# A two-layer graph network with residual norms: the gates' layer norm cut in two, evictions and copies dealt out anew, and a tile of its own for row sums

## The chip, the cores and the metric

The kernel runs on one core of a Trainium2 chip. The core has a matrix engine (TensorE, PE in the profile), a vector engine (VectorE, DVE), a scalar engine (ScalarE, ACT), GpSimd (POOL) and a sync engine (SyncE, SP) that here only issues transfers. Each engine works through its own queue of instructions in order. The metric is the device time of one launch in microseconds (us), as the median of several runs; lower is better.

## The reference

There are 64 graphs of 256 nodes with 256 features, all in float32. Two layers follow each other, each with a residual sum and a layer norm without gain and bias:

```python
# layer 0
deg = adj.sum(-1);  d = where(deg != 0, deg, 1) ** -0.5
h   = (d[:, :, None] * adj * d[:, None, :] + alpha * eye) @ x
x   = layernorm(x + h @ W.T + b)

# layer 1, with mask = adj
h      = relu(bn1(conv1(x)));  h = bn2(conv2(h))        # conv2 has 17 taps along the nodes
x_conv = relu(h + x)
s      = x @ w_se.T + b_se                              # 3 columns
A      = exp(-|s_n - s_m|^2) * adj
x_nmp  = A @ relu(x @ w_msg.T + b_msg)
gi, gh = [x_conv, x_nmp] @ w_ih.T + b_ih,  x @ w_hh.T + b_hh
r, z   = sigmoid(gi_r + gh_r), sigmoid(gi_z + gh_z)
n      = tanh(gi_n + r * gh_n)
x      = layernorm(x + (1 - z) * n + z * x)
```

## The kernel before, in words

The graphs are taken in four blocks of 16 (`Q` = 16, `NQ` = 4). Each graph passes three stages.

**Layers.** `layer0(g)` makes row sums of adj, its transpose, and the first layer. The row sums (`degrees()`, L356) are ScalarE copies of adj whose accumulators are kept and whose copied values go into a part of the tile `adjT` that is overwritten later; `adjT` has three buffers, and its last reader of an earlier graph is the product with the exponentials (L508). `layer1(g, place)` makes from the norm's output the transposed input `xn` (`x1_transposed`, L430 on VectorE and L431 on ScalarE, out of one PSUM bank), the first convolution (p_conv, L446), messages (L467), the forward transform of 32 + 16 node windows (p_dft, L482) into the big tile `V`, the distances (`dist_l` on ScalarE, L497, and `dist_r` on VectorE, L499, out of one bank), and the product with the masked exponentials (p_nmp, L515).

**Transform.** The 17-tap convolution of a block is done in the frequency domain. `products(step)` multiplies the block's tile by tables streamed from DRAM (p_k, L541), `real_transform`, `complex_begin` and `complex_end(q)` are the inverse transform, nearly all VectorE, which ends with transfers to `xc_d` (L729).

**Gates.** `gru(g)` makes the gates as a block product with seven multiplications (p_g, L856) whose operands are sums formed by GpSimd (`input_sums`, L838). VectorE joins the products (L873, L874, L882, L884, L921), ScalarE applies tanh (L897, L913), and `finished(part)` joins the gates with x1 and ends with the layer norm and the output transfer (L917). `layernorm` is a generator in two parts: statistics, and the power -0.5 on GpSimd (L328); then, after a `yield`, the negative mean times scale on VectorE (L331) and two ScalarE activations (L333). `layer0` uses the pause in it; `finished` does not: `run(layernorm(...))` issues both parts at once. `load_x1(g)` (L794) loads the residual into one of two buffers, from which the output is also stored. For some graphs (`in_blocks`) VectorE transposes the convolution's result (L812) and GpSimd adds to it (L813), for the others TensorE transposes it (L822).

The blocks overlap. The first graphs of a block (`AHEAD`: 12 of the second block, 6 of the third and fourth) run their layers while the block before is still in the transform. As `V` is in use by then, they write into a second tile `V2`, and `copies(V2)` moves their columns into `V` once the inverse transform is done (L1086). The 12 graphs of the second block are the set `ALONE`: no gates run beside them, and each calls `x1_transposed` for the graph after it, ahead of its own p_nmp. While the inverse transform and these graphs run together, `paced` issues pieces of the transform behind certain marked instructions at rates written by hand; `issue_after` ties an instruction behind another of its engine. Otherwise the planner of the framework orders each engine's instructions by program order and by when their inputs are ready in its own model, so an instruction may be issued before others that stand above it in the text. It also allots the buffers and places all waits; two engines that read one PSUM bank are kept apart.

The gates of 12 of a block's 16 graphs run during the next block's transform (`late`), the first four during the layers (`early`). The last block's gates have nothing beside them but the transform, and at the very end nothing.

Of the kernel before, what the change touches and what calls it, by code (L numbers as in the profile page):

```python
# [9 lines left out]
F32 = mybir.dt.float32  # L10
# [4 lines left out]
P = 128  # L15
# [11 lines left out]
def kernel(  # L27
# [63 lines left out]
    def mark(op, gates=0):  # L91
        marks.append((op.ins, gates))
# [24 lines left out]
    alpha_t = const.tile([P, 1], F32)  # L117

    vectors = const.tile([16, P], F32, name="bn_in")
    neg_half = const.tile([P, 4], F32)  # L120
    nc.vector.memset(neg_half, -0.5)
    load(0)
# [223 lines left out]
    def layer0(g):  # L346

        a_t, x_t = ain.pop(g), xin.pop(g)

        adjT = work.tile([P, NCH, 3, P], F32, name="adjT", bufs=3)  # L350
        ADJT[g] = adjT

        deg = small.tile([P, NCH], F32, name="deg")
        def degrees():
            for c in range(NCH):
                nc.scalar.activation(  # L356
                    adjT[:, c, 0:2, :].rearrange("p n q -> p (n q)"), a_t[:, c, :], AF.Copy,
                    accum_out=deg[:, c : c + 1],
                )

        if g == 1:

            with tc.issue_after(X_SCALED[0]):
                degrees()
        else:
            degrees()
        nc.vector.scalar_tensor_tensor(deg, deg, 0.0, deg, op0=ALU.is_equal, op1=ALU.add)  # L367
        dis = small.tile([P, NCH], F32, name="dis")
        nc.gpsimd.tensor_tensor(dis, deg, neg_half[:, :NCH], op=ALU.pow)  # L369
        adeg = small.tile([P, NCH], F32, name="adeg")  # L370
        nc.vector.tensor_scalar(adeg, deg, alpha_t, None, op0=ALU.mult)

        p = bank("p_adjT").rearrange("p (c n) -> p c n", c=NCH)
        for mc in range(NCH):
            for c in range(NCH):
                nc.tensor.transpose(p[:, mc, c * P : (c + 1) * P], a_t[:, c, mc * P : (mc + 1) * P], ident)
        copied = nc.scalar.copy(adjT[:, :, 0:3:2, :], p.rearrange("p c (n q) -> p c n q", q=P))
        for mc in range(NCH):  # L380
            DIAGONAL[g] = nc.vector.scalar_tensor_tensor(
                adjT[:, mc, 1, :], ident, adeg[:, mc : mc + 1], adjT[:, mc, 2 * mc, :],
                op0=ALU.mult, op1=ALU.add,
            ).ins


        x1 = work.tile([P, NCH, D], F32, name="x1")
        X1[g] = x1
        with tc.issue_after(copied.ins) if g < 2 else ExitStack():
            for c in range(NCH):  # L390
                X_SCALED[g] = nc.scalar.activation(x1[:, c, :], x_t[:, c, :], AF.Copy, scale=dis[:, c : c + 1]).ins
        nc.gpsimd.tensor_tensor(x_t, x_t, b0_t.unsqueeze(1).to_broadcast([P, NCH, D]), op=ALU.add)

        yield
        hT = work.tile([P, DCH, N], F32, name="hT", bufs=1)
        p = bank("p_hT").rearrange("p (k n) -> p k n", k=DCH)
        for k in range(DCH):
            for mc in range(NCH):
                nc.tensor.matmul(  # L399
                    p[:, k, :], x1[:, mc, k * P : (k + 1) * P],  # L400
                    adjT[:, mc, 1 - mc : 3 - mc, :].rearrange("p n q -> p (n q)"),
                    start=mc == 0, stop=mc == NCH - 1,
                )
        nc.scalar.copy(hT, p)  # L404
        yield
        p = bank("p_out0").rearrange("p (c o) -> p c o", c=NCH)
        for c in range(NCH):
            for k in range(DCH):
                nc.tensor.matmul(  # L409
                    p[:, c, :], hT[:, k, c * P : (c + 1) * P], w0[:, k, :], start=k == 0, stop=k == DCH - 1  # L410
                )
        for c in range(NCH):
            mark(
                nc.vector.scalar_tensor_tensor(
                    x1[:, c, :], p[:, c, :], dis[:, c : c + 1], x_t[:, c, :], op0=ALU.mult, op1=ALU.add
                )
            )
        yield
        yield from layernorm(x1)
        nc.scalar.dma_start(x1_d[g // Q][g % Q].rearrange("(c p) d -> p c d", p=P), x1)  # L420
        yield

    def x1_transposed(g):
        x1 = X1.pop(g)
        xn = XN[g] = work.tile([P, 2 * DCH, N], F32, name="xn")
        p = bank("p_x1T").rearrange("p (k n) -> p k n", k=DCH)
        for k in range(DCH):
            for c in range(NCH):
                nc.tensor.transpose(p[:, k, c * P : (c + 1) * P], x1[:, c, k * P : (k + 1) * P], ident)
        nc.vector.tensor_scalar(xn[:, 0], p[:, 0], others_only, unit, op0=ALU.mult, op1=ALU.add)  # L430
        nc.scalar.copy(xn[:, 2 * DCH - 1], p[:, 1])  # L431

    def layer1(g, place):
# [62 lines left out]
        dl = work.tile([64, N], F32, name="dist_l", bufs=1)  # L496
        nc.scalar.copy(dl, p[0:64, :N])  # L497
        dr = work.tile([64, N], F32, name="dist_r", bufs=1)
        nc.vector.tensor_copy(dr, p[64:P, :N])  # L499
        yield  # L500

        aT = work.tile([P, NCH, 2, P], F32, name="aT", bufs=1)
# [5 lines left out]
        mark(nc.vector.tensor_mul(aT, aT, adjT[:, :, 0:3:2, :]))  # L508
        yield
        if g in ALONE:  # L510
            x1_transposed(g + 1)
        p = bank("p_nmp").rearrange("p (k n) -> p k n", k=DCH)
        for k in range(DCH):
            for mc in range(NCH):
# [277 lines left out]
    def load_x1(g):  # L792
        OWN[g] = gate.tile([P, NCH, D], F32, name="x1_g")
        nc.sync.dma_start(OWN[g], x1_d[g // Q][g % Q].rearrange("(c p) d -> p c d", p=P))  # L794
# [35 lines left out]
    def input_sums(g, *which):  # L830
        A11, A12, A21, A22 = halves(GATE[g])
        S = SUMS.setdefault(g, {})
        for i in which:
# [3 lines left out]
            }[i]  # L837
            nc.gpsimd.tensor_tensor(S[i], x, y, op=op)  # L838

    def gru(g):  # L840


# [19 lines left out]
        def quarter(c, h):  # L862
            return G[:, c, h].rearrange("p t d -> p (t d)")
# [13 lines left out]
        yield  # L877
        if following:
            transposed(g + 1)
        load_x1(g)  # L880
        p5 = product(S[1], T1)
        mark(nc.vector.tensor_add(quarter(1, 1), quarter(1, 1), p5), 1)  # L882
# [18 lines left out]
        def finished(part):  # L901
            both = G[:, part].rearrange("p c h t d -> p (c h) t d")
            chunks = both.shape[1] // 2
            r, z, n, i = (both[:, :, j, :] for j in (GR, GZ, GN, GI))
            nc.vector.scalar_tensor_tensor(n, r, 1.0, n, op0=ALU.add, op1=ALU.mult)  # L905
            i4 = i.rearrange("p (c h) d -> p c h d", h=2)
            bias = bn_t.rearrange("p (h d) -> p h d", h=2).unsqueeze(1).to_broadcast([P, chunks, 2, HD])
            nc.vector.tensor_tensor(i4, i4, bias, op=ALU.add)
            nc.vector.scalar_tensor_tensor(i, n, 0.5, i, op0=ALU.mult, op1=ALU.add)
            y = x1[:, part]  # L910
            yq = y.rearrange("p c (h d) -> p (c h) d", h=2)
            mark(nc.vector.scalar_tensor_tensor(yq, z, 3.0, yq, op0=ALU.add, op1=ALU.mult), 1)
            nc.scalar.activation(i, i, AF.Tanh)  # L913
            nc.vector.scalar_tensor_tensor(i, z, 1.0, i, op0=ALU.subtract, op1=ALU.mult)
            nc.vector.tensor_sub(yq, yq, i)
            run(layernorm(y, 4 * LN_EPS))
            nc.scalar.dma_start(out[g].rearrange("(c p) d -> p c d", p=P)[:, part], y)  # L917

        if g == B - 1:
            finished(slice(1, 2))  # L920
        mark(nc.vector.tensor_add(quarter(0, 1), quarter(0, 1), p5), 1)  # L921
        squashed(0)
        finished(slice(0, 1 if g == B - 1 else NCH))
# [27 lines left out]
    def run(stage):  # L951
        for _ in stage:
            pass
# [103 lines left out]
    def gates(q, part):  # L1057

        for i in part:
            if i == 0:  # L1060
                load_conv(q * Q)
                load_gate(q * Q)
                yield
                load_conv(q * Q + 1)
                sent(q * Q)
                yield
                transposed(q * Q)
                yield
                input_sums(q * Q, 3, 1, 2, 4)
                yield  # L1070
            yield from gru(q * Q + i)
# [8 lines left out]
    def copies(V2):  # L1080

        waiting = list(AWAY)
        AWAY.clear()
        TILES[0] = V
        for i in waiting:
            nc.scalar.copy(V[:, :, :, i * GT : (i + 1) * GT], V2[:, :, :, i * GT : (i + 1) * GT])  # L1086
            yield

    late = nothing()
    for q in range(NQ):  # L1090
# [32 lines left out]
        if more:  # L1123
            run(late)
            run(end)
            if q == 0:
                scope.close()
                gate = ctx.enter_context(tc.tile_pool(name="gate", bufs=2))
            early = gates(q, range(EARLY))
            others = [take(early, 5 if q == 0 else 2) for _ in range(Q)]  # L1130
            run(graphs(first, range(AHEAD, Q), others))
            run(early)
            if q == 0:
                scope, AHEAD, V2 = open_ahead(6)
                ctx.enter_context(scope)
            late = gates(q, range(EARLY, Q))
        else:
            run(gates(q, range(Q)))
    order.close()


# [51 lines left out]
```

## Time and profile before

| | before |
|---|---|
| time, median of 3 runs | 2126.97 us (2122.22 to 2134.46) |
| the profiled execution | 2127.71 us, of which span 2125.9 us |
| TensorE busy (matmuls) | 2006.1 us, 94% of the span |
| VectorE busy | 1474.1 us, 69% |
| ScalarE busy | 905.3 us, 43% |
| GpSimd busy | 666.8 us, 31% |
| HBM, mean over the span | 139 GB/s |

The span is the time from the first to the last instruction of the program. Busy time counts the stretches in which an engine has at least one instruction running; matmuls overlap one another. A line such as L430 is a line of the kernel's file, printed with the functions above. "p_conv L446 <- DVE xn L430" says that the instruction on the left waited for the one on the right.

### The profile page before, as it was taken

To read this page: it belongs to the slowest core of one execution; us is meant where nothing else is said; L and a number is where in the kernel's file an instruction comes from. 1 tells how busy PE (TensorE), PEld (TensorE's weight loads), DVE (VectorE), ACT (ScalarE), POOL (GpSimd) and SP (SyncE) were. 2 spreads that over 40 slices of the span, in tenths; PEclk is the share of its full clock that TensorE was granted. 3 is DMA by queue.
4 is the path that set the end of the run, shared out by engine and by line. 5 is a ranking of instruction groups with operands and counts; after the bars stand their busy time and mean duration, and the time that the engine had idled before them with its cause. 6 is when DMAs were issued, how large, how long until landed. Compare 5 with 4: busy or idle time off the path is not lost. (4 is left out here: it accounts for less than half of the span.)

```text
span 2125.9 us, 26260 instructions
## 1 busy us (share of the span) xinstructions
PE 2006.1 (94%) x8157; PEld 1443.2 (68%) x8157; DVE 1474.1 (69%) x3347; ACT 905.3 (43%) x2114; POOL 666.8 (31%) x672
## 2 busy tenths in 40 slices
PE   6999999888999999999999999999999999899997
PEld 5888788766667756667777666667777765555554
DVE  5555567775558788774556888875445889977776
ACT  4666643456432234555553123446554123233333
POOL 3445310121431243223321234323232123344443
PEclk9999999999999999999999999999999999999999
DMA  4766556433437645344335655334323754443331
GB/s 125 230 210 200 192 183 209 154 132 119 122 96 226 194 123 139 114 120 120 94 99 179 201 155 140 118 104 134 96 93 100 243 146 131 111 118 95 93 94 56
DMA packets 305289, 298.05 MB, mean 140 GB/s; under 512 B 84192, under 2 KB 283956, under 8 KB 305150
## 3 DMA queue, kind: packets, MB, share of 16 engines
q1 hardware_dynamic: 245198, 200.37, 32.1%
q10 hardware_dynamic: 44480, 67.39, 8.9%
q0 software_dynamic: 15472, 28.61, 6.0%
q8 instruction: 66, 1.08, 0.2%
q14 instruction: 73, 0.60, 0.1%
HBM read 193.19 MB, written 103.06 MB: 139 GB/s over the span
## 5 line engine op out<-in xcount | busy, mean ns | idle before, releaser
L856 PE MATMUL p_g<-wall,sums 128*128 128x384 f32 x1536 | 537.7, 489 | 11.6 <-DVE G L882 11.6
L856 PE MATMUL p_g<-wall,inputs 128*128 128x384 f32 x1152 | 409.4, 492 | 14.5 <-DVE G L874 14.1
L856 PEld LDWEIGHTS p_g<-wall,sums 128*128 128x128 f32 x1536 | 284.6, 191 | 200.3 <-issue 19.1
L856 PEld LDWEIGHTS p_g<-wall,inputs 128*128 128x128 f32 x1152 | 218.5, 192 | 167.5 <-DVE G L874 23.4
L838 POOL TENSOR_TENSOR sums<-inputs 128x384 f32<-128x384 f32 x128 | 139.9, 1093 | 343.2 <-PE p_g L856 296.9
L369 POOL TENSOR_TENSOR dis<-deg,neg_half 128x2 f32<-128x2 f32 x64 | 48.3, 754 | 475.7 <-DVE deg L367 468.6
L897 ACT ACTIVATE G<-G 128x512 f32<-128x512 f32 x128 | 80.7, 630 | 250.8 <-DVE G L884 148.6
L328 POOL TENSOR_TENSOR ln_rs<-ln_rs,neg_half 128x2 f32<-128x2 f32 x129 | 94.9, 736 | 275.1 <-DVE ln_rs L327 226.7
L541 PE MATMUL p_k<-u,VM 128*128 128x256 f32 x736 | 175.8, 381 | 4.1 <-DMA u<-ud 4.1
L541 PEld LDWEIGHTS p_k<-u,VM 128*128 128x128 f32 x736 | 139.4, 191 | 31.3 <-DMA u<-ud 3.9
L446 PE MATMUL p_conv<-wc,xn 128*128 128x259 f32 x512 | 130.4, 392 | 22.7 <-DVE xn L430 21.5
L399 PE MATMUL p_hT<-adjT,x 128*128 128x256 f32 x512 | 126.7, 391 | 15.6 <-ACT msg L470 8.2
L333 ACT ACTIVATE x_g<-x_g,ln_mr,ln_rs 128x256 f32<-128x256 f32 x128 | 70.0, 593 | 150.3 <-DVE ln_mr L331 148.3
L446 PEld LDWEIGHTS p_conv<-wc,xn 128*128 128x128 f32 x512 | 94.2, 191 | 53.1 <-DVE xn L430 31.1
L508 DVE TENSOR_TENSOR aT<-aT,adjT 128x512 f32<-128x512 f32 x64 | 44.8, 699 | 123.0 <-ACT aT L507 122.8
L409 PE MATMUL p_out<-w,hT 128*128 128x256 f32 x512 | 123.7, 384 | 3.4 <-ACT hT L404 3.0
L482 PE MATMUL p_dft<-fwd,h 128*128 128x240 f32 x512 | 117.4, 372 | 9.2 <-ACT scols L450 8.8
L515 PE MATMUL p_nmp<-aT,msg 128*128 128x256 f32 x512 | 122.6, 383 | 0.7 <-DVE aT L508 0.7
L467 PE MATMUL p_msg<-wmsg,xn 128*128 128x256 f32 x512 | 122.0, 381 | 0.0
L838 POOL TENSOR_TENSOR sums<-inputs,sums 128x384 f32<-128x384 f32 x64 | 70.2, 1097 | 161.3 <-PE p_g L856 160.6
L331 DVE SCALAR_TENSOR_TENSOR ln_mr<-ln_mv,ln_rs 128x2 f32<-128x2 f32 x129 | 47.3, 368 | 101.7 <-POOL ln_rs L328 101.7
L409 PEld LDWEIGHTS p_out<-w,hT 128*128 128x128 f32 x512 | 95.6, 190 | 29.9 <-ACT hT L404 9.9
(160 smaller groups left out, 3642.0 us busy)
## 6 DMA issues: line engine op xcount, KB each, us to landing
u<-ud SPq DMA_DIRECT2D x284, 256.0 KB
xn_d<-xn ACTq DMA_DIRECT2D x64, 512.0 KB
inputs<-xn_d SPq DMA_DIRECT2D x64, 512.0 KB
ud<-u_set POOLq DMA_DIRECT2D x39, 480.0 KB, 6.3
adj_t<-in_adj_dram SPq DMA_DIRECT2D x64, 256.0 KB
x_t<-in_x_dram SPq DMA_DIRECT2D x64, 256.0 KB
x_d<-x ACTq DMA_DIRECT2D x64, 256.0 KB
xc_d<-VM SPq DMA_DIRECT2D x64, 256.0 KB
```

The source lines that it names most:

```text
L328: nc.gpsimd.tensor_tensor(rs[:, : len(chunks)], rs[:, : len(chunks)], neg_half[:, : len(chunks)], op=ALU.pow)
L333: nc.scalar.activation(y[:, c, :], y[:, c, :], AF.Identity, bias=mr[:, c : c + 1], scale=rs[:, c : c + 1])
L399: nc.tensor.matmul(p[:, k, :], x1[:, mc, k * P : (k + 1) * P], adjT[:, mc, 1 - mc : 3 - mc, :].rearrange("p n q -> p (n q)"), start=mc == ...
L409: nc.tensor.matmul(p[:, c, :], hT[:, k, c * P : (c + 1) * P], w0[:, k, :], start=k == 0, stop=k == DCH - 1)
L446: nc.tensor.matmul(p, x1T[:, k, c * P : (c + 1) * P], wc1[:, k, :], start=k == 0, stop=k == DCH - 1)
L467: nc.tensor.matmul(p[:, c, :], x1T[:, k, c * P : (c + 1) * P], wmsg[:, k, :], start=k == 0, stop=k == DCH - 1)
L482: nc.tensor.matmul(p[:, t0 * FL : t1 * FL], h[:, c, k * P : (k + 1) * P], fwd[:, first : first + t1 - t0, :].rearrange("p t f -> p (t f)") ...
L515: nc.tensor.matmul(p[:, k, :], msg[:, mc, k * P : (k + 1) * P], aT[:, mc].rearrange("p n q -> p (n q)"), start=mc == 0, stop=mc == NCH - 1,)
L541: nc.tensor.matmul(p[:, j * D : (j + 1) * D], v[:, k, :], u[:, k, :], start=k == 0, stop=k == DCH - 1)
L838: nc.gpsimd.tensor_tensor(S[i], x, y, op=op)
L856: nc.tensor.matmul(p[:, : 3 * HD] if k == 0 else p[:, HD:], a[:, k], wall[:, b, k].rearrange("p t d -> p (t d)"), start=first and k == 0, ...
L897: nc.scalar.activation(rz, rz, AF.Tanh, scale=0.5)
```

## The change

It has four parts. The row sums of adj write their unused copy into a tile of their own. In the graphs of `ALONE`, `x1_transposed` and the copy `dist_r` use ScalarE for the eviction that VectorE did. Of the copies from `V2` to `V`, every second one goes to VectorE. And the gates' layer norm is a generator `normed`, of which `finished` runs the first part; `ended()` runs what is left, together with the output transfer, from the next graph's gates, from the last graph between its two halves, and once after all.

```diff
     vectors = const.tile([16, P], F32, name="bn_in")
+    unused = const.tile([P, N], F32, name="unused")
...
         def degrees():
             for c in range(NCH):
                 nc.scalar.activation(
-                    adjT[:, c, 0:2, :].rearrange("p n q -> p (n q)"), a_t[:, c, :], AF.Copy,
+                    unused, a_t[:, c, :], AF.Copy,
                     accum_out=deg[:, c : c + 1],
                 )
...
-    def x1_transposed(g):
+    def x1_transposed(g, alone=False):
...
-        nc.vector.tensor_scalar(xn[:, 0], p[:, 0], others_only, unit, op0=ALU.mult, op1=ALU.add)
+        if alone:
+            nc.scalar.activation(xn[:, 0], p[:, 0], AF.Identity, bias=unit, scale=others_only)
+        else:
+            nc.vector.tensor_scalar(xn[:, 0], p[:, 0], others_only, unit, op0=ALU.mult, op1=ALU.add)
         nc.scalar.copy(xn[:, 2 * DCH - 1], p[:, 1])
...
-        nc.vector.tensor_copy(dr, p[64:P, :N])
+        if g in ALONE:
+            nc.scalar.copy(dr, p[64:P, :N])
+        else:
+            nc.vector.tensor_copy(dr, p[64:P, :N])
...
         if g in ALONE:
-            x1_transposed(g + 1)
+            x1_transposed(g + 1, True)
...
+    NORMS = []
+
+    def normed(g, part, y):
+
+        yield from layernorm(y, 4 * LN_EPS)
+        nc.scalar.dma_start(out[g].rearrange("(c p) d -> p c d", p=P)[:, part], y)
+
+    def ended():
+        while NORMS:
+            run(NORMS.pop(0))
+
     def gru(g):
...
         if following:
             transposed(g + 1)
+        ended()
         load_x1(g)
...
-            run(layernorm(y, 4 * LN_EPS))
-            nc.scalar.dma_start(out[g].rearrange("(c p) d -> p c d", p=P)[:, part], y)
+            NORMS.append(normed(g, part, y))
+            next(NORMS[-1])

         if g == B - 1:
             finished(slice(1, 2))
+            ended()
...
         for i in waiting:
-            nc.scalar.copy(V[:, :, :, i * GT : (i + 1) * GT], V2[:, :, :, i * GT : (i + 1) * GT])
+            copy = nc.vector.tensor_copy if i % 2 else nc.scalar.copy
+            copy(V[:, :, :, i * GT : (i + 1) * GT], V2[:, :, :, i * GT : (i + 1) * GT])
             yield
...
             run(gates(q, range(Q)))
+    ended()
     order.close()
```

## The prediction

> **What bounds the kernel now.** I read the busy shares first, then the windows by stage, then TensorE's waits inside the stages that lose time, and last the timeline of those places.
>
> ```profile
> span 2125.9 us, 26260 instructions
> ...
> PE 2006.1 (94%) x8157; PEld 1443.2 (68%) x8157; DVE 1474.1 (69%) x3347; ACT 905.3 (43%) x2114; POOL 666.8 (31%) x672
> ```
>
> TensorE is the bound: the whole change can win only what TensorE stands idle, 2125.9 - 2006.1 = 119.8 us. The first 50 us hold 50 - 32.4 = 17.6 us of it (loads and setup) and the tail after the last matmul 26.0 - 14.5 = 11.5 us. Neither is touched, so 90.7 us in the middle are at stake, 4% of the span. The windows (columns: window, its length, busy time of PE, PEld, DVE, ACT, POOL with instruction counts, clock, DMA) say where:
>
> ```profile
> 410.00:514.00 104.00, 91.16 (x444) 72.89 (x443) 79.60 (x233) 57.51 (x157) 20.73 (x22) 1.00 0.38 128
> 514.00:524.00 10.00, 3.87 (x18) 3.08 (x18) 0.62 (x5) 10.00 (x18) 0.89 (x2) 0.78 0.28 94
> 1745.00:1900.00 155.00, 140.94 (x440) 81.16 (x441) 140.13 (x271) 47.62 (x87) 58.80 (x59) 0.98 0.46 123
> 1900.00:2100.00 200.00, 197.85 (x612) 115.62 (x611) 144.84 (x264) 73.37 (x132) 95.65 (x104) 1.00 0.37 92
> ```
>
> The graphs of layers that run ahead (410 to 514) lose 12.8 us, the ten microseconds after them 6.1 us with ScalarE busy for all ten, the last block's gates under the inverse transform (1745 to 1900) 14.1 us with VectorE at 90%. The last fifteen gates (1900 to 2100) lose only 2.1 us. The waits of TensorE from 290 to 550 (total us, times, longest) name the late engine:
>
> ```profile
> PE p_conv L446 <- DVE xn L430: 12.5, 8, 3.1
> PE p_dft L482 <- ACT scols L450: 6.1, 1, 6.1
> PE p_hT L399 <- DVE adjT L381: 4.1, 5, 1.5
> PE p_dist L506 <- DVE dist_r L499: 2.7, 5, 1.1
> ```
>
> One such graph in the timeline (start, duration, engine, line):
>
> ```profile
> 437.29 0.42 ACT L356 ACTIVATE adjT<-adj_t 128x256 f32<-128x256 f32 x1 [0.76 <-DVE aT L508]
> 437.54 0.60 PE L429 MATMUL p_x1T<-ident,x 128*128 128x128 f32 x4
> 437.97 1.89 PE L515 MATMUL p_nmp<-aT,msg 128*128 128x256 f32 x8
> 439.90 0.59 ACT L519 COPY xn<-p_nmp 128x512 f32<-128x512 f32 x1 [1.70 <-PE p_nmp L515]
> 441.42 0.54 DVE L430 TENSOR_SCALAR xn<-p_x1T,others_only,ident 128x256 f32<-128x256 f32 x1
> 441.99 0.37 ACT L431 COPY xn<-p_x1T 128x256 f32<-128x256 f32 x1 [1.50 <-DVE xn L430]
> 442.01 0.70 PE L446 MATMUL p_conv<-wc,xn 128*128 128x259 f32 x2 [2.15 <-DVE xn L430]
> ```
>
> The transposes end at 438.14, but L430 stands 3.3 us behind transform work on VectorE; ScalarE idles 1.70 us meanwhile. The 6.1 us wait is the shared copies:
>
> ```profile
> 514.61 8.17 ACT L1086 COPY VM<-V 128x768 f32<-128x768 f32 x11
> 523.16 1.17 PE L482 MATMUL p_dft<-fwd,h 128*128 128x240 f32 x2 [6.13 <-ACT scols L450]
> ```
>
> From 1745 to 1900 TensorE waits for VectorE's gate sums, and VectorE itself for GpSimd's power:
>
> ```profile
> PE p_g L856 <- DVE G L874: 7.7, 4, 3.1
> PE p_g L856 <- DVE G L882: 6.9, 5, 2.1
> ...
> DVE ln_mr L331 <- POOL ln_rs L328: 5.6, 10, 2.1
> ```
>
> [...] L431 waits for L430 in all 12 run-ahead graphs, 14.6 us in sum. [...]
>
> **The change part by part.**
>
> *Copies.* Twelve copies take 513.87 to 522.78, 0.74 us each; six go to VectorE, which has 0.62 us of work in that window. ScalarE is free 6 x 0.74 = 4.5 us earlier, and the 6.1 us gap falls to 1.6. One copy on VectorE costs [...] 0.93 [...] worked out from the two-input rows of 512 elements (0.66) and 1152 (1.35). Six make [...] 5.6 us, so if all wait for the slower the gain is 6.1 - 2.7 = 3.4. If the two engines are made to take turns, the twelve need 6 x (0.74 + 0.93) = 10 us and the gap grows by 1. Later blocks have five copies each with no TensorE wait on them: 0. **Taken 4.5, ends -1 and 6.**
>
> *ScalarE's evictions in run-ahead graphs.* Twelve graphs lose L430 (536 ns) and L499 (426 ns) on VectorE, 11.5 us. ScalarE gains an Identity with two [128,1] operands, 0.56 us (382 + 2 x 90, the step from L449 to L507), and a 0.37 us copy like L497: 11.2 us on top of 57.5 in 104. In the graph shown 0.56 + 0.37 = 0.93 fits in ScalarE's 1.70 us, and p_conv starts when p_nmp ends: 2.15 us won. The seven waits of this kind before 514 sum to 9.6 us; I take 7.5, as ScalarE will sometimes be in a longer instruction. Of the 2.7 us at p_dist I take 1.5 (a cross-engine handoff goes, the second eviction still follows the first), of L381's 4.1 us 1.0 for the lightened VectorE. **Taken 10**, top 16.4. Bottom: ScalarE late by 0.5 us in all twelve where VectorE was no worse, -6. Late next is L381, and the 2.9 us wait at 536, whose graph is not a run-ahead one.
>
> *Row sums to their own tile.* Nothing is added: 128 activations of 409 ns with their 187 ns readouts remain. What goes is the wait of L356 for L508 (34.9 us, 43 times). ScalarE idles 57% of the span, so the wait itself costs little; it holds what is queued behind: L391, L519, L449, L470. TensorE's waits for ScalarE outside the copies are 8.2 (msg), 2.7 (scols) and 3.0 (hT) us, 13.9, and half would be a good result. Against it, these 0.9 us a graph stood in a gap of ScalarE (437.3 to 438.2 above); issued earlier they can stand ahead of an eviction. **Taken 0, ends -10 and 7.**
>
> *Norm in two parts.* Instruction count is the same: 65 ends of L331, two L333 (1.09 us a pair) and an output DMA (0.38 us on ScalarE's queue) move behind the next graph's L873, L874 and transposes. L331 idles VectorE 101.7/116 = 0.88 us on average, 0.56 from 1745 to 1900, with L874 behind it. TensorE waits for L874 nine times where gates meet the transform (7.7, 2.0 from 640 to 850, 3.9 from 1150 to 1350). L331 stays ahead of L882, so those waits remain, and where L874 was late from transform work the gain is partial: 9 x 0.56 = 5.0, **taken 3**, top 9 x (0.88 + 0.16, L331 itself) = 9. Bottom: SP's x1 load (L794) waits for the output that frees its buffer (219.2 us, 56 times) and holds the later loads of xc blocks and the one-row inputs on SP, for which GpSimd's L813 waits (60.9 us), then the sums. An output 1 us later in six of the last gates without slack: -6. The tail is written out at once for the last graph: 0. GpSimd's own order is unchanged.
>
> Sum: 4.5 + 10 + 0 + 3 = 17.5 us. From the profiled execution's 2127.7 us (span 2125.9 and 1.8 around it) to 2110.2; the median of the three runs is 0.7 lower, which makes 2109.5, rounded to **2110**.
>
> **Rivals.** *The gaps move.* VectorE is 77% busy from 410 to 514 and must finish the inverse transform before the copies; when TensorE arrives earlier, L381 and L414 are late instead. For: its work falls by only 8 x 0.96 = 7.7 us there. Against: ScalarE and VectorE both idle over 20%. Then only the copies and a third of the rest remain, 4.5 + 4 = 8.5: 2118, chance 0.22, and with it the case that the planner, which issues by readiness, leaves the norm's end where it was.
>
> *Row sums in the way.* ScalarE is in order. L356, free of L508, is ready as soon as adj is loaded, and 0.9 us of it can land in front of hT (L404), msg or the exponentials in some 61 graphs. For: TensorE already waits for ScalarE 13.9 us with p_hT and p_out directly behind. Against: TensorE usually has a product in between. In half of the graphs it costs 30 x 0.9 = 27 us, net 2110 + 27 = 2137 to 2140; the point where it eats the gain is 19 graphs. Chance 0.15, slower.
>
> **The numbers.** Forecast 0.63. A measurement here tells about 0.5% (10.6 us) from no change: faster is below 2116, slower above 2138. The range reaches from 2095 (copies 6, evictions 14, norm 6, row sums 6) to 2135, into the slower rival's lower end.
>
> **What would show it.** Right: the wait of p_dft on scols near 520 under 2 us; p_conv on xn before 514 under 3 us; L356 without a wait for L508; TensorE idle near 100 us; L331 hardly waiting for GpSimd in the gates. Wrong: new TensorE waits for hT, msg or aT on ScalarE, L1086 copies strictly by turns, or L794 waiting longer with L813 behind it.

## The result, and the profile after

The changed kernel takes 2115.7 us (median of 9 runs, 2108.9 to 2121.4); the kernel before takes 2131.4 us beside it. The ratio is 0.9926, 95% interval [0.9909, 0.9942]: 15.7 us faster, where 17.5 were predicted. (The 2110 us of the prediction start from the 2127.0 on record; beside the changed kernel the kernel before took 4.4 us more.) The two profiled executions show less, 2125.9 against 2119.6 us of span, because this one of the changed kernel is the slowest of its nine and that of the kernel before among its faster ones. Single stages are therefore compared below, not the spans. The lines of the changed kernel stand 1 to 21 lower in the code: L357 makes the row sums, L432 and L504 are ScalarE's new evictions, L1107 the copies.

First the busy shares of the kernel after:

```profile
PE 2012.2 (95%) x8157; PEld 1448.3 (68%) x8157; DVE 1463.9 (69%) x3333; ACT 906.1 (43%) x2128; POOL 671.3 (32%) x672
```

TensorE stands idle for 2119.6 - 2012.2 = 107.4 us, 12.4 less than before. The windows of the kernel after (window, length, busy time of PE, PEld, DVE, ACT, POOL, clock, DMA share, GB/s) show where; the line for 200 to 300 is new:

```profile
200.00:300.00 100.00, 87.48 (x397) 70.49 (x396) 49.32 (x128) 50.12 (x134) 30.20 (x28) 0.93 0.47 145
...
410.00:514.00 104.00, 99.76 (x483) 81.19 (x483) 76.89 (x237) 71.61 (x188) 23.84 (x23) 0.98 0.42 140
514.00:524.00 10.00, 8.50 (x45) 7.21 (x44) 7.57 (x21) 8.88 (x19) 1.94 (x2) 1.00 0.44 140
1745.00:1900.00 155.00, 144.14 (x459) 83.23 (x460) 145.38 (x284) 49.86 (x92) 66.83 (x64) 1.00 0.48 124
```

The graphs that run ahead now lose 4.2 us where they lost 12.8. The ten microseconds at the copies lose 1.5 where they lost 6.1, with VectorE at 7.57 us instead of 0.62. The last block's gates lose 10.9 where they lost 14.1. But 200 to 300 us loses 12.5, and the same window of the kernel before only 4.2:

```profile
200.00:300.00 100.00, 95.83 (x466) 79.90 (x465) 57.56 (x148) 56.41 (x147) 30.90 (x29) 0.98 0.56 179
```

TensorE's waits from 290 to 550 in the kernel after (total us, times, longest). The 12.5 us for xn on VectorE have become 0.6, the 6.1 for scols 1.5:

```profile
PE p_dist L513 <- ACT dist_r L504: 2.3, 2, 1.8
PE p_dft L486 <- ACT scols L454: 1.5, 1, 1.5
PE p_hT L400 <- DVE adjT L382: 1.1, 3, 0.5
PE p_conv L450 <- DVE xn L434: 0.6, 1, 0.6
```

The timeline of the kernel after has one run-ahead graph, and then the copies:

```profile
502.34 1.89 PE L522 MATMUL p_nmp<-aT,msg 128*128 128x256 f32 x8
502.55 0.57 ACT L432 ACTIVATE xn<-p_x1T,ident,others_only 128x256 f32<-128x256 f32 x1 [2.01 <-PE p_x1T L430]
...
504.07 1.91 PE L450 MATMUL p_conv<-wc,xn 128*128 128x259 f32 x8
...
517.96 3.77 ACT L1107 COPY VM<-V 128x768 f32<-128x768 f32 x5
518.49 2.89 DVE L1107 COPY VM<-V 128x768 f32<-128x768 f32 x6
522.12 1.89 PE L486 MATMUL p_dft<-fwd,h 128*128 128x240 f32 x8 [1.50 <-ACT scols L454]
```

L432 runs as soon as the transposes end, and p_conv follows p_nmp without a gap, as the prediction drew it. Both engines copy at the same time, not by turns.

The loss before 300 us begins in ScalarE's queue. First the group of the row sums in the kernel after (busy us, mean ns, idle time before them and what ended it), then the place:

```profile
L357 ACT ACTIVATE unused<-adj_t 128x256 f32<-128x256 f32 x128 | 53.4, 417 | 45.4 <-DMA adj_t<-in_adj_dram 41.0 <-DMA bn_in<-in_bn_v_dram 3.1
```

```profile
249.75 0.39 SPq L108 DMA_DIRECT2D adj_t<-in_adj_dram  x1
...
250.44 1.89 PE L471 MATMUL p_msg<-wmsg,xn 128*128 128x256 f32 x8
251.29 1.12 ACT L334 ACTIVATE x<-x,ln_mr,ln_rs 128x256 f32<-128x256 f32 x2
257.65 0.42 ACT L357 ACTIVATE unused<-adj_t 128x256 f32<-128x256 f32 x1 [5.23 <-DMA adj_t<-in_adj_dram]
...
258.06 0.58 ACT L474 ACTIVATE msg<-p_msg 128x512 f32<-128x512 f32 x1
...
258.69 3.78 PE L400 MATMUL p_hT<-adjT,x 128*128 128x256 f32 x8 [4.53 <-ACT msg L474]
```

The wait for L508 (34.9 us before) is gone, and a wait of 41.0 us for the row sums' own load has taken its place. The load leaves at 249.75, and ScalarE stands in front of it from 252.4 to 257.65. The msg eviction, whose product ended at 252.3, is queued behind it: it starts at 258.06, and TensorE stands 4.53 us. The last line also shows what follows: p_hT takes 3.78 us for 8 pieces, from 258.69 to 262.47 us, where the granted clock is 0.50. At a clock of 1.00 it takes 1.89 (at 483.58 us).

### The profile page after: what moved, and what is told of

Read it like the earlier page. It is cut to its first block, busy times and chain, and to the rows that moved or that the text cites. A ratio compares the mean times of both kernels' runs of the same rounds, so it can differ in the third digit from the quotient of the medians.

```text
span 2119.6 us, 26193 instructions
## 1 busy us (share of the span) xinstructions
PE 2012.2 (95%) x8157; PEld 1448.3 (68%) x8157; DVE 1463.9 (69%) x3333; ACT 906.1 (43%) x2128; POOL 671.3 (32%) x672
## 5 line engine op out<-in xcount | busy, mean ns | idle before, releaser
L874 PE MATMUL p_g<-wall,sums 128*128 128x384 f32 x1536 | 538.8, 491 | 7.2 <-DVE G L901 7.2
L874 PE MATMUL p_g<-wall,inputs 128*128 128x384 f32 x1152 | 407.4, 490 | 14.3 <-DVE G L892 14.3
L874 PEld LDWEIGHTS p_g<-wall,sums 128*128 128x128 f32 x1536 | 285.2, 191 | 197.5 <-issue 16.7
L874 PEld LDWEIGHTS p_g<-wall,inputs 128*128 128x128 f32 x1152 | 217.2, 191 | 166.8 <-DVE G L892 23.8
L393 POOL TENSOR_TENSOR x_t<-x_t,b_t 128x512 f32<-128x512 f32 x64 | 94.4, 1476 | 135.8 <-issue 111.4
L486 PE MATMUL p_dft<-fwd,h 128*128 128x240 f32 x512 | 117.0, 372 | 11.2 <-ACT scols L454 11.2
L400 PEld LDWEIGHTS p_hT<-adjT,x 128*128 128x128 f32 x512 | 96.0, 198 | 27.9 <-ACT msg L474 10.9
```

The costliest lines, as they stand in the source:

```text
L400: nc.tensor.matmul(p[:, k, :], x1[:, mc, k * P : (k + 1) * P], adjT[:, mc, 1 - mc : 3 - mc, :].rearrange("p n q -> p (n q)"), start=mc == ...
L486: nc.tensor.matmul(p[:, t0 * FL : t1 * FL], h[:, c, k * P : (k + 1) * P], fwd[:, first : first + t1 - t0, :].rearrange("p t f -> p (t f)") ...
L874: nc.tensor.matmul(p[:, : 3 * HD] if k == 0 else p[:, HD:], a[:, k], wall[:, b, k].rearrange("p t d -> p (t d)"), start=first and k == 0, ...
```

## The experiments

All ratios are to the kernel before on the same chip, with 95% intervals; 0.001 is 2.1 us. Two ratios of about +-0.002 differ by their difference +-0.003, that is +-6 us. So single parts are known to about 5 us, and the stages of the profile have to say the rest.

**One part taken out of the kernel after**, four runs. The copies all on ScalarE:

```diff
-            copy = nc.vector.tensor_copy if i % 2 else nc.scalar.copy
+            copy = nc.scalar.copy
```

> The changed kernel (ratio to before 0.9926, 15.7 us less) with all copies from V2 to V on ScalarE again. Theory A (the prediction's terms hold): the wait of p_dft on scols near 520 comes back from 1.5 to about 6 us, so 4.5 us of the gain go: 11.2 us less than before, ratio 0.9947. Rival (the gaps move: the freed 4.5 us are lost again behind the next late instruction): ratio stays at 0.993 within 0.001.

Measured: 2125.6 us, 0.9969 [0.9953, 0.9985]. The shared copies are worth 9 +- 5 us, where 4.5 were predicted. That alone would not exclude 4.5; the stage that holds the copies is 11.4 us longer (below).

The evictions of the run-ahead graphs back on VectorE:

```diff
-            x1_transposed(g + 1, True)
+            x1_transposed(g + 1)
...
-        if g in ALONE:
-            nc.scalar.copy(dr, p[64:P, :N])
-        else:
-            nc.vector.tensor_copy(dr, p[64:P, :N])
+        nc.vector.tensor_copy(dr, p[64:P, :N])
```

> The changed kernel with L430 and L499 of the run-ahead graphs on VectorE again. Theory A: the 10 us of this part go, 5.7 us less than before remain, ratio 0.9973, with p_conv waiting on xn for some 9 us again before 514. Rival (the part is worth more, since from 290 to 520 TensorE stood idle only 5 us after the change and 22 before with the copies' 6): 13 to 15 us go, ratio 0.999 to 1.000.

Measured: 2138.7 us, 1.0032 [1.0019, 1.0045]. Beside the other three parts the evictions are worth 23 +- 5 us, not 10. TensorE's waits in this kernel's run-ahead graphs (405 to 530 us) begin with the old one, larger than ever:

```profile
PE p_conv L450 <- DVE xn L434: 14.0, 7, 3.7
```

The row sums into adjT again:

```diff
-                    unused, a_t[:, c, :], AF.Copy,
+                    adjT[:, c, 0:2, :].rearrange("p n q -> p (n q)"), a_t[:, c, :], AF.Copy,
```

> The changed kernel with the row sums' unused copy in adjT again, so that L357 waits for L515 (the product with the exponentials, L508 before). Theory A (row sums are worth nothing): ratio 0.993. Theory B (the row sums, issued ahead of their load, hold ScalarE's queue: in the profile after, L357 waits 41.0 us for the load of adj, 10.1 of them from 200 to 300, where TensorE lost 7.6 us more than before): the wait for the load goes, TensorE gets back 7 to 10 us, ratio 0.988 to 0.9895. Rival C (the wait removed was worth something elsewhere): slower than the changed kernel, 0.995.

Measured: 2108.7 us, 0.9885 [0.9866, 0.9904]. In the full change the row sums' own tile costs 9 +- 5 us. In this kernel the window from 200 to 300 us is as full as before the change:

```profile
200.00:300.00 100.00, 95.83 (x474) 80.16 (x473) 58.28 (x153) 58.05 (x151) 30.93 (x30) 1.00 0.58 186
```

The norm in one piece at its old place:

```diff
-            NORMS.append(normed(g, part, y))
-            next(NORMS[-1])
+            run(normed(g, part, y))
```

> The changed kernel with both parts of the gates' norm run at once. Theory A: the 3 us of this part go, ratio 0.994, TensorE's waits for the gate sums L892 and L901 rise from 21.5 us towards 25.7. Rival (the planner issues the second part as soon as it is ready in both, so the order hardly changes): ratio 0.9926 within 0.001.

Measured: 2133.1 us, 1.0002 [0.9985, 1.0018]. Beside the other parts the later end is worth 16 +- 5 us, not 3. The four parts by removal come to 9 + 23 - 9 + 16 = 39 us and the whole change to 15.7, so the parts are not independent.

**Parts alone.** The kernel before with only the row sums' tile, and the kernel after with only copies and evictions (row sums in adjT, norm at once; both edits shown above):

> The kernel before with the row sums' discarded products in a tile of their own, nothing else. Theory A (ScalarE is held at its own load wherever the row sums are free to be issued early): slower by 6 to 13 us, ratio 1.003 to 1.006, and L357 waits 25 us or more for adj_t's load. Theory B (the row sums only cost because the run-ahead evictions came to ScalarE in the same stage): no difference, ratio 0.999 to 1.001. The prediction's own term: 0, within -10 to +7 us.

> Shared copies and ScalarE's evictions alone: no tile for the row sums, the gates' norm at once. Against the run without the row sums' edit (0.9885) it prices the norm's later end where no row sum is ahead of its load. Theory A (the later end is worth about 16 us by itself, as beside the other three edits): ratio 0.996 to 0.998. Theory B (half of the 16 us came from the row sums, which the norm at once delayed further): ratio 0.991 to 0.994. The prediction's term of 3 us would give 0.990.

Measured: row sums alone 2164.0 us, 1.0159 [1.0134, 1.0184], 34 us slower. Copies and evictions alone 2110.9 us, 0.9918 [0.9889, 0.9947], 17.5 +- 6 us faster where the prediction had 14.5. From there to the kernel without the row sums' edit (0.9885) the norm adds 7 +- 7 us. So without the early row sums the terms of the prediction for copies, evictions and norm hold within what can be measured. The larger figures by removal were all measured beside early row sums.

The stages say where. Each column is one profiled execution (of "copies + evictions" the fastest of its six, of "row sums only" the slowest of its six). The first row ends with the first product (p_real) of the first block's transform, the second with the transform's last product; three of the graphs run ahead lie between these products. The third row holds the other nine and ends with their last p_dft, and each row after it ends with the first p_real of the next block:

| stage, us | before | after | copies + evictions | the same + norm | row sums only | row sums early in run-ahead graphs only |
|---|---|---|---|---|---|---|
| first block's layers | 282.7 | 298.8 | 281.1 | 282.9 | 296.7 | 281.4 |
| transform products | 101.1 | 100.7 | 100.7 | 100.7 | 101.1 | 100.7 |
| graphs run ahead | 121.8 | 109.9 | 113.6 | 113.6 | 130.3 | 107.6 |
| rest of block 2's layers, copies in it | 130.2 | 121.0 | 119.3 | 121.7 | 135.6 | 120.4 |
| to block 3's first p_real | 502.4 | 508.3 | 506.6 | 507.7 | 515.0 | 510.3 |
| to block 4's first p_real | 502.7 | 504.4 | 501.4 | 504.6 | 506.1 | 501.3 |
| to the last product | 473.6 | 464.9 | 469.5 | 464.4 | 474.6 | 464.7 |

The early row sums cost 12 to 19 us in the first block: it takes 294.5 to 299.9 us in the nine kernels of this study with early row sums throughout, and 281.1 to 282.9 in the other five. In the graphs run ahead they cost 8.5 us beside VectorE's evictions (121.8 to 130.3) and gain 3 to 6 beside ScalarE's (113.6 to between 107.6 and 110.8). The norm's later end gains 5 us in the last block (469.5 to 464.4) and nothing, or a small loss, before it.

**Is it the load?** A third load buffer for adj_t, then the loads reordered as well:

```diff
-        ain[g] = loads.tile([P, NCH, N], F32, name="adj_t")
-        nc.sync.dma_start(ain[g], adj[g].rearrange("(c p) m -> p c m", p=P))
+        for a in ((0, 1) if g == 0 else (g + 1,)):
+            if a < B:
+                ain[a] = loads.tile([P, NCH, N], F32, name="adj_t", bufs=3)
+                nc.sync.dma_start(ain[a], adj[a].rearrange("(c p) m -> p c m", p=P))
```

> The kernel after, with a third load buffer for adj_t, so that a graph's adjacency is asked for a graph earlier (the discarded row sums are bfloat16 and a set-up tile shares a slot, to make room). Theory A (the row sums cost time because ScalarE's in-order queue stands at L357 until its own load lands): the 41 us of idle ScalarE before L357 on adj_t<-in_adj_dram fall below 15 us, and the ratio to the kernel before goes from 0.9926 toward that without the row sums' edit, 0.988 to 0.990. Theory B (the row sums cost by being placed earlier, ahead of evictions, whatever they wait for): the load wait goes, the ratio stays 0.991 to 0.994, and TensorE's waits for p_dist<-dist_r and msg stay. Theory C (what counts is the traffic of the loads): the earlier load collides with the gates' weights and the ratio is above 0.994.

> The kernel after, with each adjacency asked for one graph earlier: on SP's queue adj_t of the next graph now stands ahead of x_t of this one (a third adj_t buffer, bfloat16 for the discarded row sums, a shared slot in the set-up make room). In the kernel after, SP stands 334 us at x_t's load for the read of the old x_t at L415, with adj_t's load behind it. Theory A (ScalarE's row sums lose time because their load is held behind x_t's on SP): L357's 41 us of waiting for adj_t fall below 12 us, the first product of the transform starts near 283 to 286 us and not at 299, ratio to the kernel before 0.984 to 0.989. Theory B (the row sums' place in ScalarE's queue costs, not their load): the wait goes, the first product stays near 295 us or later, ratio 0.991 to 0.994.

Measured: 2114.4 us, 0.9930 [0.9906, 0.9953], and 2114.1 us, 0.9926 [0.9909, 0.9942]. Neither helps, and neither takes the wait of 41.0 us away (40.9 and 38.0 us), so they do not decide between the theories as meant. This group is of the kernel with reordered loads:

```profile
L359 ACT ACTIVATE unused<-adj_t 128x256 bf16<-128x256 f32 x128 | 53.4, 417 | 43.3 <-DMA adj_t<-in_adj_dram 38.0 <-DMA bn_in<-in_bn_m_dram 3.9
```

The reason is the order of ScalarE's instructions in the traces. Here it is for graph 9 (counted from 0): when its row sums start, and when the evictions of p_adjT that come behind them start, with their graph:

```
                   row sums    evictions behind them
before             141.73      150.04 (graph 9)
after              127.24      136.42 (graph 8), 152.07 (graph 9)
loads reordered    115.50      124.19 (graph 7), 139.84 (graph 8), 155.50 (graph 9)
```

From the seventh graph on it is the same for every graph, and the third load buffer alone gives the order of the reordered loads. In the kernel before, the wait for L508 kept each graph's row sum next to that graph's own eviction. Free of it, the planner, which issues by readiness, puts the row sum a graph ahead. With an earlier load it moves a further graph ahead, and again it stands right behind its load (issued 233.58, row sum 240.14, in the timeline of the kernel with reordered loads):

```profile
233.58 0.38 SPq L110 DMA_DIRECT2D adj_t<-in_adj_dram  x1
240.14 0.42 ACT L359 ACTIVATE unused<-adj_t 128x256 bf16<-128x256 f32 x1 [3.54 <-DMA adj_t<-in_adj_dram]
```

So place and wait come together in these runs, but not everywhere. In the kernel after, the row sums of six graphs stand at the early place between 100 and 200 us. Two of their twelve instructions wait for a load, 0.8 us in sum, and TensorE loses nothing:

```profile
100.00:200.00 100.00, 100.00 (x500) 83.98 (x499) 54.52 (x129) 65.21 (x168) 51.82 (x48) 1.00 0.66 210
```

The next twelve, from 200 to 300 us, wait 10.1 us in three places, and there TensorE loses its time. So in the first block the early place costs nothing where the load is there in time.

**Row sums early only where they gain**, in the graphs that run ahead. `layer0` is two graphs ahead of `layer1`, so these are the row sums of graphs 18 to 29:

```diff
-                    unused, a_t[:, c, :], AF.Copy,
+                    unused if g - 2 in ALONE else adjT[:, c, 0:2, :].rearrange("p n q -> p (n q)"),
+                    a_t[:, c, :], AF.Copy,
```

> The kernel after, with the row sums' own tile used only for the graphs of layers that run ahead (graphs 18 to 29), and adjT for all others. Theory A (the early row sums lose 12 to 16 us in the first sixteen graphs, with the gates' weights being loaded, and gain 4 to 6 us in the graphs run ahead): first product at 281 to 284 us, graphs run ahead 108 to 110 us long instead of 113.6, ratio 0.985 to 0.987. Theory B (the graphs run ahead are only shorter because what they need was done in the longer first stage): they stay at 112 to 114 us, ratio 0.988 to 0.990.

Measured: 2101.3 us, 0.9873 [0.9851, 0.9894], the lowest time of the study, 27 us below the kernel before and 11 +- 6 below the kernel after (0.9926). Against the kernel without early row sums (0.9885) it is 3 +- 6 us, which the totals do not tell from nothing; the stage does. The last column of the table has its stages: the first block is as short as before, and the graphs run ahead take 107.6 us. What they gain shows in TensorE's waits there. First the kernel with all row sums in adjT, then this one:

```profile
PE p_hT L399 <- DVE adjT L381: 6.7, 7, 2.0
```

```profile
PE p_hT L401 <- DVE adjT L383: 1.7, 4, 0.6
```

The diagonal (L381, L383) needs the row sums, which VectorE multiplies by alpha. An earlier row sum takes most of that wait away. Its own waits cost little here: of the 8.5 us that the 24 early row sums wait for their loads, 7.5 come before this stage, under the transform's products, where TensorE is busy 100.6 of 100.7 us.

**The norm's end still later**, behind the next product's add, without the row sums' edit:

```diff
-        ended()
         load_x1(g)
...
         mark(nc.vector.tensor_add(quarter(1, 0), quarter(0, 1), p7), 1)
+        ended()
```

> Without the row sums' edit, and with the norm's end put behind the next product's eviction of the gates (behind the quarter(1,0) add) and not ahead of load_x1. Theory A (the waits of the add and of the first eviction on the norm's GpSimd step are what is left to gain): the 11 us of TensorE's waits at the two adds in the gates fall to 7 or less and the ratio goes from 0.9885 to 0.984 to 0.987. Theory B (TensorE's waits there move to the next eviction): ratio 0.987 to 0.990. Theory C (the later end holds ScalarE in front of the layers' h and scols): above 0.991.

Measured: 2108.2 us, 0.9892 [0.9867, 0.9918], no difference. TensorE's waits for the two adds in the last block stay at 13.2 us (7.0 and 6.2) against 12.7. But the edit changed next to nothing: in the two traces the instructions of TensorE, VectorE and GpSimd and the transfers of SyncE come in the same order, and ScalarE's differ in the place of one msg eviction. The planner, which issues by readiness, put the norm's end at the same place again. So the run does not decide between its theories; it measures the same order twice.

**Why the copies are worth more than their gap.** With all copies on ScalarE the rest of block 2 takes 132.4 us, 11.4 more than in the kernel after. TensorE's idle time is 7.2 of it (14.5 against 7.3), and its busy time for the same products grows by the other 4.2 (117.9 against 113.7). Of the idle time 4.4 us are the gap (5.9 against 1.5), and 2.0 are the next wait for xn, 0.6 us in the kernel after:

```profile
PE p_conv L450 <- DVE xn L434: 2.6, 1, 2.6
```

The windows show the clock, last column but two. It is at half in two stretches, one that begins 2.3 us into the gap (514.1 to 520.0) and one behind the wait at 530.3 us:

```profile
516.40:523.20 6.80, 3.18 (x8) 2.75 (x9) 1.03 (x5) 6.70 (x16) 0.00 (x0) 0.50 0.19 31
523.20:533.50 10.30, 7.61 (x38) 5.86 (x38) 5.44 (x14) 3.98 (x11) 2.94 (x4) 1.00 0.65 145
533.50:536.90 3.40, 3.40 (x12) 2.72 (x11) 0.61 (x2) 1.54 (x4) 0.47 (x1) 0.50 1.02 367
```

TensorE is busy for 3.2 and 3.4 us of them. The p_dft right behind the gap takes 3.46 us for 8 pieces, where it takes 1.89 in the kernel after. At half the speed the two stretches account for an estimated 3.3 us of the 4.2, half of their busy time. So half speed followed a gap of 5.9 us and a wait of 2.6 us alike.

Two runs filled the gap with products of resident tiles whose result nobody reads, put just ahead of it, 20 and then 12 of them (all copies on ScalarE, as in the run above):

```diff
-            copy(V[:, :, :, i * GT : (i + 1) * GT], V2[:, :, :, i * GT : (i + 1) * GT])
+            made = copy(V[:, :, :, i * GT : (i + 1) * GT], V2[:, :, :, i * GT : (i + 1) * GT])
+            if AHEAD == 12 and i == waiting[3]:
+                p = bank("p_fill")
+                with tc.issue_after(made.ins):
+                    for _ in range(12):
+                        nc.tensor.matmul(p[:, :D], ident, wmsg[:, 0, :], start=True, stop=True)
```

> The kernel after with all twelve copies on ScalarE (where TensorE stands 5.9 us at the transform's p_dft), and with 20 products of 128x256 of resident tiles, whose result nobody reads, put on TensorE just ahead of the p_conv before that gap: about 4.8 us of work where TensorE would stand. Theory A (a gap of that length brings the granted clock down for the next microseconds, which is why the copies on ScalarE cost 9 us and not the 4.6 of the gap): granted clock from the end of the run-ahead graphs to the second block's first transform product 0.98 or more where it was 0.94, that stage 3 to 5 us shorter, ratio 0.994 to 0.996. Theory B (the clock falls whatever TensorE does there, or the rest of the 9 us is a wait elsewhere): clock 0.93 to 0.95, ratio 0.9965 to 0.999.

> As the run with 20 products in the gap, with 12 of them: one took 0.44 us (8.8 us for 20, more than the gap of 5.9), so 12 are 5.3 us. Theory A (the gap lowers the granted clock behind it, and that costs about 3 us beside the gap itself): granted clock 1.00 from 510 to 550 us, TensorE's busy time in the stage up to the second block's first transform product 2 to 3 us above the 117.9 of the kernel without products although 5.3 us of work are added, the stage 2.5 to 3.5 us shorter than 132.4, ratio 0.994 to 0.996. Theory B (the clock is lower there for another reason): busy time 123 us, the stage as long as before, ratio 0.997 to 0.999.

Measured with 20: 2125.0 us, 0.9977 [0.9966, 0.9989]. With 12: 2125.7 us, 0.9977 [0.9957, 0.9997]. The windows from 510 to 540 us with 12:

```profile
510.00:520.00 10.00, 9.81 (x49) 8.07 (x49) 4.81 (x13) 7.44 (x18) 1.93 (x2) 1.00 0.44 145
520.00:530.00 10.00, 8.57 (x44) 7.28 (x43) 1.03 (x5) 9.91 (x19) 0.00 (x0) 1.00 0.20 50
530.00:540.00 10.00, 8.91 (x44) 6.74 (x43) 4.65 (x15) 5.12 (x15) 2.61 (x3) 1.00 0.66 156
```

The clock stays at 1.00, and the stage is 128.4 us long instead of 132.4 (129.3 with 20 products), although TensorE does 5.3 (8.8) us more. In this kernel the p_dft waits 1.4 us and the next p_conv 0.6. So with the gap filled and the second wait down from 2.6 us to 0.6, both stretches of half speed are gone (1.00 for 0.50): that the clock falls here behind TensorE's standing still is shown. That the filling saves time in the whole is not: both totals equal the 2125.6 without it, and an expected 3 to 4 us is within what these runs differ.

## Why the prediction was right, point by point

**The total held, in part by luck.** The predicted gain was 4.5 + 10 + 0 + 3 = 17.5 us against 15.7. In the order of the experiments the terms measure 17.5 +- 6 for copies and evictions (14.5 predicted), 7 +- 7 for the norm (3) and -9 +- 5 for the row sums (0). So a loss that was put at nothing is offset by parts that came out somewhat above their terms. What the sum had right is the main mechanism: TensorE's waits behind VectorE's evictions and behind the copies, and how to shorten them. What it had wrong are the row sums, the price of a gap, and the place where the norm gains.

*Evictions.* The term of 10 us was for the graphs run ahead. The table has 121.8 - 113.6 = 8.2 us for nine of them and 101.1 - 100.7 = 0.4 for the stage with the other three. The picture of one graph, L432 in ScalarE's gap and p_conv right after p_nmp, came as drawn, with 0.57 us for L432 against the 0.56 worked out from 382 ns for L449 and 472 for L507. The 23 us by removal belong to a kernel that the prediction did not price: with early row sums and VectorE's evictions, TensorE waits 14.0 us for xn and its granted clock is 0.93 in this stage, where the kernel after has 0.98, and of the 20.5 us by which that kernel's run-ahead graphs are longer (130.4 to 109.9) 7.4 are slower products.

*Copies.* The gap went from 6.1 to 1.50 us (1.6 predicted). That 4.5 was taken and not 3.4 needs a VectorE copy faster than the 0.93 us worked out from two-input rows. This was the author's estimate, which no trace of the kernel before shows; in the kernel after the copy takes 549 ns, and VectorE's six end at 521.38, ScalarE's at 521.73. The taking of turns that was the bad end did not come. The price failed at one step, the equation of a gap with its length: the stage also held a wait of 2 us more for xn and 4.2 us of slower products.

*Row sums.* The prediction took 0 with an end of -10, and the measured -9 lies at that end. The rival "Row sums in the way" had the right place, ahead of msg on ScalarE, and the wrong price. It charged 0.9 us of work in each of 30 graphs, 27 us. The kernel after shows waits of up to 5.2 us for a load, six of them: 11.6 us in all before 300 us. TensorE's new waits there are 5.0 us for msg and 3.3 for dist_r; the first is one of the wrong signs that the prediction named, though over the whole program the waits for msg fall from 8.2 to 6.2 us. From 200 to 300 us the granted clock is 0.93 for 0.98, and of the 15.9 us by which the first block is longer than without early row sums (298.8 against 282.9), 6.8 are slower products. The sentence "the wait itself costs little" looked at the wait that goes and not at the next one, the load, behind whose issue the row sum starts 7.9 us later in the kernel after (6.6 with reordered loads). In the full change the rival did not come in its size; alone, on the kernel before, it did: the same edit costs 34 us there, far beyond the end of -10. The table shows the difference in the graphs run ahead, where the early row sum costs 8.5 us beside VectorE's evictions and gains 3 to 6 beside ScalarE's.

*Norm.* In the last block the later end gains 5 us. That this is also the 9 x 0.56 of the prediction is chance: those nine waits lay in three blocks, and the gain was to come at L874, with the waits for L882 to remain. Over the whole program it is the other way round. The pages of the kernel before and after (after the last bar: TensorE's idle time before these products, and what ended it):

```profile
L856 PE MATMUL p_g<-wall,sums 128*128 128x384 f32 x1536 | 537.7, 489 | 11.6 <-DVE G L882 11.6
L856 PE MATMUL p_g<-wall,inputs 128*128 128x384 f32 x1152 | 409.4, 492 | 14.5 <-DVE G L874 14.1
```

```profile
L874 PE MATMUL p_g<-wall,sums 128*128 128x384 f32 x1536 | 538.8, 491 | 7.2 <-DVE G L901 7.2
L874 PE MATMUL p_g<-wall,inputs 128*128 128x384 f32 x1152 | 407.4, 490 | 14.3 <-DVE G L892 14.3
```

From 1745 to 1900 us the waits for the two adds fall from 14.6 to 11.2 us; the kernel after:

```profile
PE p_g L874 <- DVE G L892: 7.6, 7, 1.6
PE p_g L874 <- DVE G L901: 3.6, 4, 1.7
```

The order of VectorE's instructions in the traces says why so little moved. The prediction had L874 behind L331. But the kernel before already has the norm's end behind the next graph's L874 in 31 of 63 graphs, the kernel after in 35; of those after 1723 us only two were still ahead of it. So the second half of the rival "The gaps move", that the planner leaves the end where it was, came true for most graphs as far as L874 goes, where half of the ends were behind it from the start. The two ends that did move behind L874 in the last block account for most of its 5 us: in the kernel with copies and evictions TensorE waits 3.1 and 2.5 us for L874 at these places, and 1.5 and 1.1 with the later end, and a stretch of half speed of 3.4 us behind the first is gone (TensorE is busy 371.8 us from the transform's last product to its own last, and 370.1 with the later end).

The sign "L331 hardly waiting for GpSimd in the gates" did not come: it waits 3.6 us instead of 5.6 there and 91.3 instead of 101.7 in all. The wrong sign "L794 waiting longer" came, 219.2 to 233.3 us (now L801), without a loss: GpSimd's wait for the inputs behind it fell from 60.9 to 45.8 us.

*The rest.* The signs for p_dft, p_conv and L508 came. TensorE's 107.4 us of idle time is between the 119.8 before and the 100 expected.

**What stays open.** Block 3 gives back 4 to 12 us in every faster variant (506.6 to 514.4 us against 502.4), at different waits in each. In the kernel with copies, evictions and norm, part of it is p_dft's wait for scols. There ScalarE stands 4.63 us at a layer's norm with h and scols behind it:

```profile
1012.02 1.09 ACT L333 ACTIVATE x<-x,ln_mr,ln_rs 128x256 f32<-128x256 f32 x2 [4.63 <-DVE ln_mr L331]
1013.02 0.36 ACT L452 ACTIVATE h<-p_conv 128x256 f32<-128x256 f32 x1
...
1013.48 0.30 PEld L485 LDWEIGHTS p_dft<-fwd,h 128*128 128x128 f32 x2 [2.31 <-ACT scols L453]
```

Why the norm at once costs 16 +- 5 us beside early row sums and 7 +- 7 without them is only narrowed down. Block 3 has 12.4 us of it (520.7 against 508.3), of which 8.0 are slower products; in blocks 3 and 4 ScalarE's wait at the gates' norm (x_g for ln_mr) is 74.0 us with it and 45.4 in the kernel after. And the last block is 4 us shorter with copies and evictions (473.6 to 469.5), though neither acts there.

## What to carry to other kernels

A wait that is removed from an instruction can be replaced by the next one of the same instruction, as 34.9 us for L508 were by 41.0 us for a load: look up when its other operand lands, and what would then stand behind it (TensorE for 4.53 us here). Taking away a buffer dependency also takes away a place in the order, so it can be given only to the stage that needs it, as the kernel with the lowest time here does. A gap of TensorE can cost more than its length, as slower products followed some of the gaps here (3.46 us for 1.89 behind 5.9 us). Removing one part from a finished change does not give what it would bring alone: the four removals came to 39 us and the whole to 15.7. And before an order is changed in the text, look up in the trace which order the planner has made already.

## What the runs showed of the hardware that was not expected

The slow-down behind gaps is not small change. With row sums alone, the graphs run ahead have hardly more idle time than in the kernel before (17.1 against 16.4 us). But the granted clock is 0.93 instead of 1.00, and TensorE is busy 113.2 us instead of 105.4 for the same products. The kernel after with VectorE's evictions has the same two figures, 0.93 and 113.3.

The length of the single wait does not tell when this happens. In that last kernel five stretches at half the clock, 3.4 us each, begin 2.6 to 4.2 us after the start of waits of 3.7, 3.1, 2.4, 2.4 and 1.9 us for xn. The first and the last of them:

```profile
411.44:414.85 3.41, 3.41 (x12) 2.73 (x11) 0.69 (x5) 1.81 (x6) 0.71 (x1) 0.51 0.00 0
520.67:524.08 3.41, 3.41 (x12) 2.85 (x11) 1.00 (x5) 2.15 (x7) 0.71 (x1) 0.51 0.36 101
```

In the kernel before, waits of 3.1 and 2.2 us for xn in the same stage are followed by none: the clock is 1.00 from 395 to 415 us and from 436 to 514. What decides between the two stays open; that half speed followed waits as short as 1.9 us is what these runs show.
